# Softmax totals spread through DRAM, and layer-norm tiles moved to other units, in an attention and LoRA kernel

## The chip, the cores and the metric

The kernel runs on one core of a Trainium2 chip. The metric is the time of one execution on the device, in microseconds (us). A core has five engines that run side by side, each through its own list of instructions in order: TensorE (PE; PEld is its loading of weights), VectorE (DVE), ScalarE (ACT), GpSimd (POOL) and SyncE (SP). Here SP issues every transfer (DMA). An engine waits where its next instruction needs something that another has not finished, and everything behind that instruction waits too.

## The reference

Input x has 4 sequences of 1024 rows with 1024 columns, all in 32-bit floats. Two blocks are applied, each with a layer norm in front and the input added behind:

```python
x = x + attn(layernorm(x), wq, wk, wv, wo)      # 32 heads of 32 columns, rotary q and k, causal softmax
x = x + ffn(layernorm(x), route_w, A, Bw)       # best of 8 experts, each a low-rank pair of rank 16
```

In the attention, `probs = softmax(scores)`, `out = probs @ v`, and `out @ wo`. The kernel leaves the division by the softmax's totals until after `probs @ v`: it works with unnormalized exponentials and multiplies the result by the reciprocal of each query's total.

## The kernel before

**Units.** The work is cut into 32 units, eight per sequence (`units`, line 207). A unit is four heads of one sequence: 128 columns of q, k and v. During a unit, its scores, exponentials and products with v are made, and between these the matmuls that fill TensorE: the projections of q, k and v for the next unit, and, from the second sequence on, the output projection and the second block of one tile of 128 rows of the sequence before (`finish_steps`, line 656). Units 0 to 7 are the first sequence.

**Slots.** A unit runs through eleven slots (`SLOTS`, line 26). Nine of them make scores of some query tiles (`score_round`, 64 queries each, tile 15 the longest). Two of them, "second" and "first", make the products with v (`apply`, line 981): "second" for the later half of the queries of the unit before (block 1), "first" for the earlier half of the queries of this unit (block 0). After each slot, `fill` takes steps from `todo` up to a share of their cost; a projection step costs 1 and takes 0.86 us. The fillers of unit u are the list `between[u]`. Steps of cost 0 stand in the same list and are issued when they are reached. `postponed` (line 224) holds actions that are due after so much further cost.

**Softmax on VectorE.** Per query tile: scores are copied from PSUM to SBUF by ScalarE (L417), POOL adds the mask on the diagonal (L420), VectorE finds the largest of each row (L438, L459), ScalarE exponentiates (L467), and VectorE transposes in blocks of 32x32 (L492). The products `av` (L573) need all the transposes of their block. `av` lies in the same PSUM tile as the scores (`ps_s`, one buffer), so the next scores wait until VectorE has multiplied `av` by the reciprocals (L593).

**The totals.** `join_sums` (line 525) adds two halves of the totals (L534) and takes reciprocals (L535). For each of 512 queries and 4 heads there is one number, with queries on the partitions; `av` has head columns on the partitions and queries along the row. So POOL copies each number 32 times side by side (`by`, 128x512, L537). `spread_sums` (line 542), called after the `av` matmuls have been issued, turns `by` by four TensorE transposes (L547), and ScalarE copies the result from PSUM (L548). `join_sums` is called as soon as the last transposes of the block have been issued, a slot before the products.

**Layer norm.** `Norm` (line 233) holds the eight row tiles of one sequence: `load` brings a tile, `find` computes mean and variance on VectorE (L175 to L179) and one power on POOL (L181), `scale` normalizes in place on VectorE (L186), `turn` transposes with eight TensorE transposes and copies to `xnT` (L198 to L202). For the second sequence this happens in units 5 to 7: tiles 0 to 4 are loaded at the head of unit 5; tiles 0 and 1 are scaled in unit 5, 2 to 5 in unit 6, 6 and 7 in unit 7 (lines 855 to 865 and 808 to 810). In the class, `scale(t)` for the first sequence finds tile t + 1 before it scales tile t; for the second it finds t + 1 after.

**The DMA queue.** All transfers stand in SP's one queue in program order: chunks of weights (`load_chunk`, four buffers, each load issued after the use that frees its buffer), `vd` (v written to DRAM and read back in another layout, `spread_values`, line 500), x, results. The queue stops at the first transfer whose source or buffer isn't ready.

Of the kernel before, what the change touches and what calls it, by code (L numbers as in the profile page):

```python
# [14 lines left out]
P = 128  # L15
# [56 lines left out]
def tile_preln_attn_then_top1_lora(  # L72
# [50 lines left out]
    nc.sync.dma_start(eye_sb, eye)  # L123

    def load_x(b, t, tag="row"):
        xr = big.tile([P, D], F32, tag=tag, name=f"x_{b}_{t}", bufs=COUNT[tag])
        nc.sync.dma_start(xr, x[b, t * P : (t + 1) * P, :])
        return xr
# [7 lines left out]
    x_first = [load_x(0, t) for t in range(2)]  # L136
# [25 lines left out]
    sign_sb = const.tile([P, 1], F32, name="sign_sb")  # L162

# [68 lines left out]

    class Norm:

# [10 lines left out]
        def load(self, *tiles):  # L245
            u = self.b * NG
            for t in tiles:
                n = self.homes.get(t)
                if not n:
                    self.x[t] = load_x(self.b, t)  # L250
                    continue
                dsts = qTs if n == "q" else kTs
                if u not in dsts:
                    dsts[u] = big.tile([P, S], F32, tag="qkT", name=f"{n}T_{u}", bufs=4)
                self.x[t] = dsts[u]
                nc.sync.dma_start(dsts[u], x[self.b, t * P : (t + 1) * P, :])
# [268 lines left out]
    def join_sums(u, blk):  # L525


        if (u, blk) in bys or any((u, t) in places for t in range(blk * QT, (blk + 1) * QT)):
            return
        den = dens.pop((u, blk)).rearrange("p (t c) h -> p c t h", c=2)  # L530
        rec = small.tile([P, TB, HG], F32, tag="rec", name=f"rec_{u}_{blk}", bufs=2)
        for i in range(P // SQ):
            rows, other = slice(i * SQ, (i + 1) * SQ), slice((i ^ 1) * SQ, ((i ^ 1) + 1) * SQ)
            nc.vector.tensor_tensor(rec[rows], den[rows, i % 2], den[other, i % 2], ALU.add)  # L534
        nc.vector.reciprocal(rec, rec)  # L535
        bys[u, blk] = by = big.tile([P, TB, P], F32, tag="by", name=f"by_{u}_{blk}")
        nc.gpsimd.tensor_copy(  # L537
            by.rearrange("p t (h d) -> p t h d", d=HD),
            rec.unsqueeze(3).to_broadcast([P, TB, HG, HD]),
        )  # L540

    def spread_sums(u, blk):

        by = bys.pop((u, blk))
        pt = bank([P, TB, P], f"pr_{u}_{blk}")
        for i in range(TB):
            nc.tensor.transpose(pt[:, i, :], by[:, i, :], eye_sb)  # L547
        nc.scalar.copy(by, pt)  # L548
        return by.rearrange("p t k -> p (t k)")
# [239 lines left out]
    def change_steps(u, norm, project, tail, held):  # L789
# [32 lines left out]
    for u, (b, g) in enumerate(units):  # L822
# [13 lines left out]
        if u + 1 < len(units) and g + 1 == NG:  # L836
# [306 lines left out]
```

## Time and profile before

| | |
|---|---|
| median of 3 runs | 2755.46 us (2751.7 to 2759.22) |
| the profiled execution | 2747.7 us |
| its span, first to last instruction | 2745.9 us |
| TensorE busy | 2682.2 us (98%) |
| VectorE busy | 2126.7 us (77%) |
| ScalarE busy | 1755.0 us (64%) |
| POOL busy | 638.1 us (23%) |
| granted TensorE clock, mean | 0.998 |
| four transposes of `by` (L547) | 64 blocks, 256 instructions, 42.2 us busy |
| ScalarE's copy of `by` (L548) | 64, 586 ns each |
| POOL's copy of `by` (L537) | 64, 612 ns each |

Busy time counts matmuls as one pipelined stretch; an instruction's own duration is longer than the time that it keeps the next one from starting. In a row of a timeline, the first number is the start in us, the second the length, and a bracket at the end is the idle time of that engine just before, with the instruction that ended it. "x3" means that three like instructions were merged into the row.

### The profile page before, as it was taken

To read this page: it belongs to the slowest core of one execution; us is meant where nothing else is said; L and a number is where in the kernel's file an instruction comes from. 1 tells how busy PE (TensorE), PEld (TensorE's weight loads), DVE (VectorE), ACT (ScalarE), POOL (GpSimd) and SP (SyncE) were. 2 spreads that over 40 slices of the span, in tenths; PEclk is the share of its full clock that TensorE was granted. 3 is DMA by queue.
4 is the path that set the end of the run, shared out by engine and by line. 5 is a ranking of instruction groups with operands and counts; after the bars stand their busy time and mean duration, and the time that the engine had idled before them with its cause. 6 is when DMAs were issued, how large, how long until landed. Compare 5 with 4: busy or idle time off the path is not lost.

```text
span 2745.9 us, 84082 instructions
## 1 busy us (share of the span) xinstructions
PE 2682.2 (98%) x35328; PEld 1322.0 (48%) x35328; DVE 2126.7 (77%) x4198; ACT 1755.0 (64%) x5033; POOL 638.1 (23%) x900
## 2 busy tenths in 40 slices
PE   8999999899999999989999999998999999999998
PEld 5444444444445444445444454444544444544445
DVE  4888889887777877887777778788777777778655
ACT  2877777876666676666666666666566666666521
POOL 2222223222222222222222222222222222222000
PEclk9999999999999999999999999999999999999999
DMA  3222232325444455551654444565255544446421
GB/s 118 52 56 56 56 94 56 78 56 150 131 135 114 121 141 142 151 171 43 175 145 122 135 110 121 149 165 146 63 157 150 138 128 128 115 119 196 129 67 55
DMA packets 448012, 317.86 MB, mean 116 GB/s; under 512 B 150289, under 2 KB 371729, under 8 KB 447633
## 3 DMA queue, kind: packets, MB, share of 16 engines
q1 hardware_dynamic: 447632, 312.47, 41.6%
q8 instruction: 278, 4.55, 0.7%
q14 instruction: 102, 0.83, 0.1%
HBM read 262.59 MB, written 49.81 MB: 114 GB/s over the span
## 4 chain that ended last, share of the span: by engine, by line
PE 80%; DVE 14%; ACT 2%; DMA 1%; POOL 1%; issue 1%; SPq 0%; POOLq 0%; DVEq 0%; ACTq 0%
PE po L690 14%; PE pq L313 14%; PE pk L313 13%; PE pv L313 12%; PE s L406 11%; PE av L573 9%; DVE top L438 4%; DVE pr L492 4%; PE ph L712 2%; PE pf L751 2%; DMA chunk<-in_wo 1%; DVE both L459 1%; PE pr L547 1%; ACT pr L417 1%; PE pt_f L198 1%
## 5 line engine op out<-in xcount | busy, mean ns | idle before, releaser
L467 ACT ACTIVATE pr<-pr,both 128x256 f32<-128x256 f32 (+15 forms) x2048 | 1045.1, 519 | 58.0 <-DVE both L459 57.9
L438 DVE TENSOR_REDUCE top<-pr 128x2 f32<-128x960 f32 (+15 forms) x768 | 651.1, 894 | 251.5 <-POOL pr L420 250.9
L417 ACT COPY pr<-s 128x640 f32<-128x640 f32 (+14 forms) x544 | 525.3, 1017 | 492.3 <-PE s L406 491.7
L492 DVE STREAM_TRANSPOSE pr<-pr 128x1024 f32<-128x1024 f32 (+11 forms) x768 | 664.3, 907 | 33.3 <-ACT pr L467 30.1
L420 POOL TENSOR_TENSOR pr<-pr,causal_sb 128x128 f32<-128x128 f32 x512 | 238.0, 472 | 1070.6 <-ACT pr L417 1062.4
L313 PE MATMUL pv<-xnT,wv 128*128 128x512 f32 x1024 | 484.1, 600 | 0.0
L313 PE MATMUL pq<-xnT,wq 128*128 128x512 f32 x1008 | 476.8, 600 | 0.6 <-ACT xnT L200 0.6
L313 PE MATMUL pk<-xnT,wk 128*128 128x512 f32 x1008 | 475.9, 601 | 0.0
L406 PE MATMUL s<-kT,qT 32*32 32x256 f32 (+4 forms) x17408 | 393.0, 385 | 10.7 <-ACT pr L417 7.2
L467 ACT ACTIVATION_READ_ACCUMULATOR pr<-pr,both 128x1 f32 x2048 | 400.8, 196 | 0.0
L690 PE MATMUL po<-chunk,attn 128*128 128x512 f32 x736 | 376.3, 597 | 4.0 <-DMA chunk<-in_wo 4.0
L406 PEld LDWEIGHTS s<-kT,qT 32*32 32x32 f32 x17408 | 187.2, 103 | 267.2 <-issue 101.8
L313 PEld LDWEIGHTS pk<-xnT,wk 128*128 128x128 f32 x1008 | 181.3, 190 | 234.8 <-issue 234.6
L313 PEld LDWEIGHTS pq<-xnT,wq 128*128 128x128 f32 x1008 | 182.6, 191 | 224.0 <-issue 221.8
L313 PEld LDWEIGHTS pv<-xnT,wv 128*128 128x128 f32 x1024 | 185.7, 190 | 217.2 <-issue 212.9
L573 PE MATMUL av<-pr,vals 64*32 64x256 f32 (+3 forms) x12288 | 273.2, 320 | 11.7 <-DVE pr L492 11.6
L573 PEld LDWEIGHTS av<-pr,vals 64*32 64x32 f32 x12288 | 215.5, 106 | 119.9 <-issue 54.5
L459 DVE TENSOR_TENSOR both<-top 32x4 f32<-32x4 f32 (+3 forms) x1152 | 213.4, 185 | 23.7
L690 PEld LDWEIGHTS po<-chunk,attn 128*128 128x128 f32 x736 | 135.2, 190 | 168.0 <-issue 149.6
L548 ACT COPY by<-pr 128x512 f32<-128x512 f32 x64 | 37.5, 586 | 260.5 <-PE pr L547 260.5
L593 DVE TENSOR_TENSOR at<-av,by 128x256 f32<-128x256 f32 x128 | 48.1, 417 | 158.1 <-ACT by L548 158.0
L690 PE MATMUL po<-wo,attn 128*128 128x512 f32 x256 | 116.7, 597 | 0.0
(87 smaller groups left out, 1705.8 us busy)
## 6 DMA issues: line engine op xcount, KB each, us to landing
chunk<-in_wo SPq DMA_DIRECT2D x368, 256.0 KB, 3.6
vals<-vd SPq DMA_DIRECT2D x256, 128.0 KB, 4.5
x<-in_x SPq DMA_DIRECT2D x58, 512.0 KB, 6.0
wq<-in_wq SPq DMA_DIRECT2D x32, 512.0 KB, 4.0
wk<-in_wk SPq DMA_DIRECT2D x32, 512.0 KB, 4.0
wv<-in_wv SPq DMA_DIRECT2D x32, 512.0 KB, 4.2
vd<-vT SPq DMA_DIRECT2D x128, 128.0 KB, 4.8
out_y<-x SPq DMA_DIRECT2D x32, 512.0 KB, 2.8
```

The lines of the kernel that those rows point to most:

```text
L313: nc.tensor.matmul(at["p"], lhsT=wt[:, c, :], rhs=xnTs[b, tb][:, c, :], start=(c == 0), stop=(c == NC - 1),)
L406: nc.tensor.matmul(sc[i * SQ : (i + 1) * SQ, h, at : at + w].rearrange("p (j k) -> p j k", k=SQ), lhsT=of_q[rows, 2 * t + half], rhs=of_k[ ...
L417: nc.scalar.copy(pr[:, :, k0 : k0 + w], sc[:, :, at : at + w])
L420: nc.gpsimd.tensor_tensor(diagonal, diagonal, causal_sb.unsqueeze(1).to_broadcast([P, HG, SQ]), ALU.add)
L438: nc.vector.tensor_reduce(top[:, k, h : h + step], places[u, t][:, h : h + step, :], AX.X, ALU.max, negate=True,)
L459: nc.vector.tensor_tensor(dst[rows], src[rows], src[other], op)
L467: nc.scalar.activation(pr[:, h, :], pr[:, h, :], AF.Exp, bias=tops[u, t][:, h : h + 1], accum_out=dens[u, t // QT][:, t % QT, h : h + 1],)
L492: nc.vector.transpose(pr, pr)
L573: nc.tensor.matmul(avs[half][h * HD : (h + 1) * HD, t0:, :], lhsT=v[rows, j, h * HD : (h + 1) * HD], rhs=rhs, start=(j == 0), stop=(j == n ...
L690: nc.tensor.matmul(st["po"], lhsT=lhsT, rhs=rhs, start=(c == start), stop=(c == stop))
L712: nc.tensor.matmul(ph, lhsT=st["ynT"][:, c, :], rhs=w[:, c - i * RA, :], start=(c == 0), stop=(c == NC - 1),)
L751: nc.tensor.matmul(pf, lhsT=st["whT"], rhs=rhs, start=True, stop=True)
```

## The change

1. From the second sequence on (24 units, 48 blocks), the reciprocals are no longer spread by POOL, TensorE and ScalarE. VectorE transposes them in blocks of 32x32 (`turned`, one 128x32 instruction), four small stores put them in DRAM (`there`, 16 rows of 128 bytes each), and four loads bring them back, each row of 512 numbers repeated on 32 partitions (`by`). Stores are due after 2.0 of further step cost, loads after 5.0; `spread_sums` issues what is still left. In the first sequence the old way stays. The reciprocals now live in one constant tile, `rec_sb`, whose unused columns are set to zero once.
2. The tiles of the second sequence are loaded, found and scaled one at a time: tiles 0 to 3 in units 1 to 4, tiles 4 and 5 in unit 5, tiles 6 and 7 in unit 6. Tiles 5 and 6 lie in two half tiles each (`Two`) in the buffers of the weight chunks. Unit 7 only turns tiles 4 to 7.
3. At the start, x's first tile is loaded ahead of the identity matrix, and `scale` for the first sequence finds the next tile after scaling; for the second sequence `scale` no longer finds the next tile.

```diff
-    nc.sync.dma_start(eye_sb, eye)
...
-    x_first = [load_x(0, t) for t in range(2)]
+    x_first = [load_x(0, 0)]
+    nc.sync.dma_start(eye_sb, eye)
+    x_first.append(load_x(0, 1))
...
+    rec_sb = const.tile([P, 2, SQ], F32, name="rec_sb")
+    nc.vector.memset(rec_sb, 0.0)
...
+                if n == "chunk":
+                    self.x[t] = Two([])
+                    for cols in (slice(0, HALF), slice(HALF, D)):
+                        part = big.tile([P, HALF], F32, tag="chunk", name=f"x_{self.b}_{t}", bufs=4)
+                        nc.sync.dma_start(part, x[self.b, t * P : (t + 1) * P, cols])
+                        self.x[t].parts.append(part)
+                    continue
...
-                self.find(k + 1 if self.b == 0 else k)
-                normalize(self.x[k], self.x[k], self.moments.pop(k))
+                self.find(k)
+                moments = self.moments.pop(k)
+                for part in getattr(self.x[k], "parts", [self.x[k]]):
+                    normalize(part, part, moments)
                 self.scaled += 1
-                if self.b == 1:
+                if self.b == 0:
                     self.find(k + 1)
...
-        den = dens.pop((u, blk)).rearrange("p (t c) h -> p c t h", c=2)
-        rec = small.tile([P, TB, HG], F32, tag="rec", name=f"rec_{u}_{blk}", bufs=2)
+        den = dens.pop((u, blk)).rearrange("p (t c) h -> p c h t", c=2)
+        rec = rec_sb[:, blk, : HG * TB].rearrange("p (h t) -> p h t", t=TB)
...
-        nc.vector.reciprocal(rec, rec)
-        bys[u, blk] = by = big.tile([P, TB, P], F32, tag="by", name=f"by_{u}_{blk}")
-        nc.gpsimd.tensor_copy(
-            by.rearrange("p t (h d) -> p t h d", d=HD),
-            rec.unsqueeze(3).to_broadcast([P, TB, HG, HD]),
-        )
+        nc.vector.reciprocal(rec_sb[:, blk, : HG * TB], rec_sb[:, blk, : HG * TB])
+        if units[u][0] == 0:
...
+            bys[u, blk] = by, None
+            return
+        turned = small.tile([P, SQ], F32, tag="recT", name=f"recT_{u}_{blk}", bufs=2)
+        nc.vector.transpose(turned, rec_sb[:, blk])
+        there = dram.tile([HG * TB, P // SQ, SQ], F32, tag="recs", name=f"recs_{u}_{blk}")
+        by = big.tile([P, TB * P], F32, tag="by", name=f"by_{u}_{blk}")
+
+        def put():
+            for i in range(P // SQ):
+                nc.sync.dma_start(there[:, i], turned[i * SQ : i * SQ + HG * TB])
+
+        def get():
+            for h in range(HG):
+                of_h = there[h * TB : (h + 1) * TB]
+                nc.sync.dma_start(
+                    by[h * HD : (h + 1) * HD],
+                    bass.AP(of_h.tensor, of_h.offset, [[0, HD], [1, TB * P]]),
+                )
+
+        left = [put, get]
+        bys[u, blk] = by, left
+        for cost in (2.0, 5.0):
+            postponed.append([cost, lambda: left and left.pop(0)()])
...
-        by = bys.pop((u, blk))
...
+        by, left = bys.pop((u, blk))
+        if left is None:
...
+        while left:
+            left.pop(0)()
+        return by
...
-        out += [*chains[:2], turning(4), scaling(6), *chains[2:6], turning(5), scaling(7)]
-        out += [*chains[6:11], turning(6), *chains[11:16], turning(7)]
-        return out + chains[16:]
+        for t, n in zip(range(TB, NT), (3, 4, 4, 4)):
+            out += [*chains[:n], turning(t)]
+            del chains[:n]
+        return out + chains
...
-                norm = Norm(b + 1, {0: (5,), 1: (6,), 2: (7,)})
+                norm = Norm(b + 1, {0: (7,)}, {5: "chunk", 6: "chunk"})
+                for t, (unit, at) in enumerate(((1, 24), (2, 24), (3, 24), (4, 24), (5, 12), (5, 36))):
+                    steps = between[unit]
+                    for k, step in enumerate((norm.load, norm.find, norm.scale)):
+                        steps.insert(at - 8 + 5 * k, Step(lambda step=step, t=t: step(t), 0.0))
+                for at, step in (
+                    (own["q", 0][0], Step(lambda norm=norm: norm.load(6), 0.0)),
+                    (own["q", 1][0], norm.finding(6)),
+                    (own["q", 1][3], norm.scaling(6)),
+                    (own["v", 1][5], norm.finding(7)),
+                    (own["v", 1][7], norm.scaling(7)),
+                ):
+                    behind(last_v, at, step)
                 for t, at in enumerate((("k", 1), ("k", 1), ("k", 1), ("v", 1))):
                     behind(last_v, own[at][(1 + 3 * t) % NC], norm.turning(t))
-                behind(last_v, own["v", 1][6], norm.scaling(5))
-                behind(last_v, own["v", 1][3], norm.finding(5))
-                behind(last_v, own["k", 0][4], norm.scaling(4))
-                behind(last_v, own["q", 1][2], norm.scaling(3))
-                behind(last_v, own["q", 0][2], norm.scaling(2))
-                for t in (1, 0):
-                    between[-2].insert(10 + 16 * t, norm.scaling(t))
-                between[-2].insert(0, Step(lambda norm=norm: norm.load(*range(TB + 1)), 0.0))
```

More of the change, by code (lines that the diff above doesn't have):

```diff
@@ L231, in do_postponed, with __init__, __getitem__ @@
                 item[1]()
+    class Two:
+        def __init__(self, parts):
+            self.parts = parts
+        def __getitem__(self, key):
+            rows, cols = key
+            k, at = divmod(cols.start, HALF)
+            return self.parts[k][rows, at : at + cols.stop - cols.start]
     class Norm:
@@ L534, in join_sums @@
             nc.vector.tensor_tensor(rec[rows], den[rows, i % 2], den[other, i % 2], ALU.add)
-        nc.vector.reciprocal(rec, rec)
-        bys[u, blk] = by = big.tile([P, TB, P], F32, tag="by", name=f"by_{u}_{blk}")
-        nc.gpsimd.tensor_copy(
-            by.rearrange("p t (h d) -> p t h d", d=HD),
-            rec.unsqueeze(3).to_broadcast([P, TB, HG, HD]),
-        )
-    def spread_sums(u, blk):
-        by = bys.pop((u, blk))
[L545 to L549, printed above, removed]
+        nc.vector.reciprocal(rec_sb[:, blk, : HG * TB], rec_sb[:, blk, : HG * TB])
@@ new lines, in join_sums @@
+        if units[u][0] == 0:
+            by = big.tile([P, TB, P], F32, tag="by", name=f"by_{u}_{blk}")
+            nc.gpsimd.tensor_copy(
+                by.rearrange("p t (h d) -> p t h d", d=HD),
+                rec.rearrange("p h t -> p t h").unsqueeze(3).to_broadcast([P, TB, HG, HD]),
+            )
[3 more added lines that the diff above has]
+        nc.vector.transpose(turned, rec_sb[:, blk])
@@ new lines, in join_sums @@
+        there = dram.tile([HG * TB, P // SQ, SQ], F32, tag="recs", name=f"recs_{u}_{blk}")
[9 more added lines that the diff above has]
+                    bass.AP(of_h.tensor, of_h.offset, [[0, HD], [1, TB * P]]),
+                )
@@ new lines, in join_sums @@
+        left = [put, get]
+        bys[u, blk] = by, left
+        for cost in (2.0, 5.0):
+            postponed.append([cost, lambda: left and left.pop(0)()])
+    def spread_sums(u, blk):
+        by, left = bys.pop((u, blk))
+        if left is None:
+            pt = bank([P, TB, P], f"pr_{u}_{blk}")
+            for i in range(TB):
+                nc.tensor.transpose(pt[:, i, :], by[:, i, :], eye_sb)
+            nc.scalar.copy(by, pt)
+            return by.rearrange("p t k -> p (t k)")
+        while left:
+            left.pop(0)()
+        return by
```

## The prediction

> **What bounds the kernel now.** I read the page first: busy times, chain, groups. Then TensorE's waits, the timeline of one steady unit, the first change of sequence, and the DMA issues. A unit is one pass of the main loop: 4 heads of one sequence; 0 to 7 are the first sequence, and each later sequence also carries the finishing matmuls of the one before.
>
> From the page:
>
> ```profile
> PE 2682.2 (98%) x35328; PEld 1322.0 (48%) x35328; DVE 2126.7 (77%) x4198; ACT 1755.0 (64%) x5033; POOL 638.1 (23%) x900
> ```
>
> TensorE is idle for 64 us of 2745.9. From its waits (total, times, longest):
>
> ```profile
> PE av L573 <- DVE pr L492: 11.6, 2, 9.1
> PE pt_a L198 <- DVE x L186: 9.8, 2, 9.1
> PE s L406 <- ACT pr L417: 7.2, 6, 1.7
> ```
>
> The 9.1 of the second row is the start; that of the first lies at 539 to 548, in unit 7. From 720 to 1110, in the second sequence's steady units (82.3 us each), TensorE has no wait at all: there, each us of its work is a us of time. The timeline of TensorE, then of VectorE, around one block of such a unit (start, us, instruction, [idle before]):
>
> ```profile
> 1421.70 2.35 PE L573 MATMUL av<-pr,vals 64*32 64x256 f32 x128
> 1423.98 0.65 PE L547 MATMUL pr<-eye_sb,by 128*128 128x128 f32 x4
> 1424.47 1.02 PE L313 MATMUL pv<-xnT,wv 128*128 128x512 f32 x2
> ```
>
> ```profile
> 1415.88 2.08 DVE L438 TENSOR_REDUCE top<-pr 128x2 f32<-128x896 f32 x2 [1.20 <-POOL pr L420]
> 1425.29 0.75 DVE L593 TENSOR_TENSOR at<-av,by 128x256 f32<-128x256 f32 x2 [2.63 <-ACT by L548]
> ```
>
> The four transposes of `by` hold TensorE from 1423.98 to 1424.47: 0.49 us (0.50 for the other block at 1465.54). The multiplication that needs them starts 1.3 us after the av matmuls end.
>
> The first sequence is different: in the second half of its units VectorE has no gap but one of 1.19 us, and TensorE sits at its heels. Unit 5 already normalizes a tile in that place (VectorE 432.20 to 434.56), and TensorE pays:
>
> ```profile
> 445.90 1.49 PE L406 MATMUL s<-kT,qT 32*32 32x384 f32 x64 [1.38 <-DVE at L593]
> 456.95 1.44 PE L406 MATMUL s<-kT,qT 32*32 32x256 f32 x64 [1.74 <-ACT pr L417]
> 548.09 5.90 PE L573 MATMUL av<-pr,vals 64*32 64x256 f32 x128 [9.05 <-DVE pr L492]
> ```
>
> A unit without that tile shows no wait and 0.92 us at the first two places. The third row is the pile-up: the tiles left for the end of units 6 and 7. What it does to the clock is in the table by stage (columns: stretch, length, busy PE, PEld, DVE, ACT, POOL, granted clock):
>
> ```profile
> 540.00:546.00 6.00, 0.00 (x0) 0.00 (x0) 5.82 (x13) 3.79 (x13) 0.37 (x2) 0.66 0.01 1
> 546.00:552.00 6.00, 3.91 (x72) 3.05 (x80) 5.85 (x14) 2.20 (x10) 2.17 (x5) 0.50 0.01 3
> ```
>
> These av matmuls take 5.90 us, where they take 3.69 at 400.42: 2.2 more.
>
> **Part 1, the totals by DRAM** (48 blocks, units 8 to 31). Removed per block: TensorE 0.495 us; a ScalarE copy (0.586); a POOL copy (0.612). 48 x 0.495 = 23.8. Five blocks lie where TensorE waits anyway (two at each change into the third and fourth sequence, and the last one): 43 x 0.495 = **-21.3**. The ScalarE copy is on no path of a steady unit: nothing. The POOL copy sits ahead of a mask that VectorE then waits for (the [1.20] above): VectorE gains that, which pays only at the two later changes, where VectorE is busy 38 of 40 us and TensorE waits 2.6, 2.3, 1.6 and 0.7. I take 1 us each, **-2** (0 to 4). Added on VectorE: a 128x32 transpose; the rows for 128x128 (0.30) and 256 (0.40) give an estimate of 0.2, hidden in a steady unit's idle.
>
> Added on SP: 4 stores of 2 KB and 4 loads of 64 KB per block, 0.33 to 0.43 us each to issue, 1.6 per group. The first store waits for VectorE, the first load for the stores' landing. No row has either transfer. Bounds for one landing, from the issues:
>
> ```profile
> chunk<-in_ra SPq DMA_DIRECT2D x24, 136.0 KB, 2.2
> vd<-vT SPq DMA_DIRECT2D x128, 128.0 KB, 4.8
> causal_sb<-in_causal SPq DMA_DIRECT2D x4, 4.0 KB, 5.8
> ```
>
> I take 2.2 for either leg. The last row is nearest in size, but it was issued behind some 4.5 MB of loads at the start; SP's later queue is mostly idle. The same round trip is in the kernel for `vd`: SP waits there 33 times, 33.2 us in all.
>
> Follow the block above. SP is free from 1415.9 (its next load waits until 1419.2), the totals are ready at 1414.9; stores issued by 1417.5, landed 1419.7. The loads come after five steps of cost, behind a weight chunk at 1420.1: issued 1420.4 to 1422.0, landed 1424.2. The av matmuls end at 1424.0, and the old path gave `by` at 1425.3: no loss. The other block: totals ready 1456.6, stores to 1458.2, landed 1460.4, loads to 1462.0, landed 1464.2; needed 1465.5. What stands behind these waits on SP is the router's chunks: the one of 1454.3 goes out at 1458.5, that of 1456.9 at 1462.3; both are used after 1466. Hidden, with about 3 us to spare.
>
> It isn't hidden in two places. At the changes in units 15 and 23 the store waits for totals ready at 1195.3 while three weight chunks, issued at 1190.3 to 1191.5, stand behind it. They go out at 1197, land 3.6 later, and TensorE wants the first at 1197.9: up to 3 us, of which I count half, since it waits for others soon after: **+3** for two. And units 8, 16 and 24 (short fills) reach the stores only at 663.8: loads land at 671.4, against 669.5 now; **+1.5** for three.
>
> Part 1: -21.3 - 2 + 3 + 1.5 = **-18.8**.
>
> [...]
>
> **Part 2, the tiles of the second sequence** (first: nothing of the amount of work changes, only the place). In units 1 to 4 each tile's find comes after VectorE's work of the 15th query tile, its scale directly behind. Adjacent pairs wait for POOL (0.67 at 409.93), so it is 3.07 us from 407.59 to 410.66. VectorE's gap of 1.19 there waits for VectorE's own totals by way of POOL, so it moves along. Unit 5 before: 2.36 us put in, TensorE lost 1.38 + 1.74 - 0.92 = 2.2. So 3.07 costs 2.9; four units **+11.6**. Bounds: 0, if the earlier place lets TensorE's idle-free first half absorb it, and 3.1 plus 2.2 of lost clock. I take the unit-5 row: same tile, same half.
>
> Unit 5 keeps two: tile 4 ahead of the av matmuls' next wait, free; tile 5 in halves late in the unit, 1.64 + 1.0, +2.5, against 0.88 + 2.2 = 3.1 now. Unit 7's stall: between 533.8 and 548 VectorE now does 4.74 + 2.35 = 7.1 us of normalizing; then only tile 7, 3.07. The stall of 9.05 falls by 4.0 to 5.0, enough to keep the 2.2 of clock, and 0.32 goes. Before: 3.1 + 9.05 + 2.2 + 0.32 = 14.7. After: 11.6 + 2.5 + 7.2 = 21.3. Part 2: **+6.6**. Moved with them: each tile's load (0.33 to 0.57 us of SP, which in the first sequence issues 17 DMAs a unit and stands idle otherwise; it lands about 6 us later, in a 12 us lead; tiles 5 and 6 as two loads of half the size), its POOL power (0.55 at 409.35, between other POOL work) and, in unit 7, the tile turns, one matmul step earlier or later: nothing each. Without that lead, VectorE would stand at the find.
>
> [...]
>
> **Part 3, the start.** x's first tile is issued at 0.74, not 1.18 (-0.4), and its scale no longer stands behind the second tile's statistics (6.60 to 8.15): scale at 6.9 instead of 8.22, so the first transposes begin at 7.8 and not 9.08. The weights follow in the old order. **-1.3** (0 to -1.8). A memset of 64 columns lies beside the first load.
>
> **Sum:** -18.8 + 6.6 - 1.3 = -13.5. The profiled execution took 2747.7 us (span 2745.9): 2734.2. The median shown is 2755.46, 7.8 above it: **2742**.
>
> **Rivals.**
> - *The moved tiles are absorbed.* Part 2 loses the 11.6: -25, 2730. For it: VectorE idles 2.8 and 3.5 us in the first half of each unit. Against it: unit 5.
> - *The stalls in units 1 to 4 drop the clock.* 4 x 2.2 on top: 2751. For it: 135.18, after 2.60 us. Against it: 1.73 and 1.74 cost no clock.
> - *Slower: the round trip by DRAM ends after the av matmuls in every unit.* VectorE then stands at the multiplication, the PSUM tile stays held, and TensorE's next scores wait. In the first block that starts when two landings take over 9.3 us (from 1417.5 with 1.6 of issue and 0.75 of multiplying to 1429.2). At 5.8 each it is 2.3 us there and 1.8 in the other block, 24 x 4.1 = 98: 2840. For it: the causal row. Against it: every large transfer of the middle lands in 2.2 to 4.8.
> - *TensorE's gain comes back as waits on VectorE or ScalarE* (no gain from part 1's slots): 2763. Against it: 77% and 64% busy.
>
> **Chances.** Forecast 0.50, absorbed 0.20, clock 0.13, slow round trip 0.12, no gain 0.05. About 0.3%, 8 us, is what a measurement can tell from no change: faster means below 2747. Of the forecast's 0.50 I put 0.08 above that. Faster 0.42 + 0.20 = 0.62; same 0.08 + 0.13 + 0.05 = 0.26; slower 0.12. The range takes in the first three cases with their bounds: 2726 to 2760.
>
> **What the new profile would show.** Steady units of 81.3 us; SP's waits for the `recs` stores 48 times, a few us each at most; VectorE's wait at the multiplication on PE or DMA, short. Units 1 to 4 with 2 to 3 us of new TensorE waits on `at` and `pr`, the stall in unit 7 at about 5. I am wrong if the multiplication waits for DMA by more than 5 us in steady units, or if units 1 to 4 keep their length.

## The result, and the profile after

| | before | after |
|---|---|---|
| median, 14 runs each | 2749.74 us (2745.66 to 2759.22) | 2750.8 us (2745.76 to 2754.09) |
| ratio | | 0.9999, 95% interval 0.9991 to 1.0007 |
| the profiled execution | 2747.7 us | 2752.48 us |
| its span | 2745.9 us | 2750.7 us |
| its granted clock, mean | 0.998 | 0.992 |

No difference that can be measured. The granted clock is the one number of the table that moved. It isn't chance: 29 runs of the kernel before lie at 0.994 to 0.998 (mean 0.9960), the 14 runs of the changed one at 0.991 to 0.994 (mean 0.9926). Taken over 2750 us, the clock lacks some 11 us per run before and some 20 after.

From the page of the changed kernel:

```profile
PE 2680.1 (97%) x35136; PEld 1307.2 (48%) x35136; DVE 2143.1 (78%) x4249; ACT 1727.5 (63%) x4985; POOL 608.5 (22%) x852
```

192 matmuls are gone, yet TensorE's busy time fell by only 2.1 us: matmuls in a drop of the clock were busy for longer, as shown below (the same 64 took 2.35 us in a drop and 1.48 at full clock).

**The steady units** are shorter, as forecast, but by 0.79 us and not by 0.99 (81.54 from 82.33). The timeline of TensorE behind the av matmuls of one block:

```profile
1510.35 2.35 PE L626 MATMUL av<-pr,vals 64*32 64x256 f32 x128
1512.63 1.13 PE L337 MATMUL pv<-xnT,wv 128*128 128x512 f32 x2
1513.59 1.02 PE L743 MATMUL po<-chunk,attn 128*128 128x512 f32 x2
```

The four transposes no longer stand between av and pv. But the first pv group now holds TensorE from 1512.63 to 1513.59, 0.96, where the like group at 1516.17 holds it 0.86 (to 1517.03). Before, the pv group behind the transposes held it 0.86 too (1424.47 to 1425.33). So here the first group after av takes 0.10 us more, and before, that lay in the transposes: they held TensorE 0.49, but only 0.39 of it goes with them.

VectorE at another block of the same unit, and what SP's queue waited for (total, times, longest):

```profile
1544.81 0.21 DVE L570 STREAM_TRANSPOSE recT<-rec_sb 128x32 f32<-128x32 f32 x1
1553.93 0.76 DVE L646 TENSOR_TENSOR at<-av,by 128x256 f32<-128x256 f32 x2 [1.52 <-PE av L626]
```

```profile
SPq L576 <- DVE recT L570: 252.8, 48, 13.0
SPq L581 <- DMA recs<-recT: 32.1, 46, 2.4
```

The multiplication waits for TensorE's av and not for the loads: the round trip is hidden, as it was worked out. From 700 to 1110 and from 1300 to 1790 TensorE has no wait. The second row is SP's wait for the stores to land, 0.7 us a block. The first is the price in the queue: SP stands 252.8 us in all before a store that VectorE hasn't made ready.

**The first sequence.** TensorE's timeline in units 1 to 5 and 7:

```profile
181.49 2.35 PE L430 MATMUL s<-kT,qT 32*32 32x384 f32 x64 [2.70 <-DVE at L646]
252.01 1.61 PE L430 MATMUL s<-kT,qT 32*32 32x384 f32 x64 [2.71 <-DVE at L646]
322.61 1.48 PE L430 MATMUL s<-kT,qT 32*32 32x384 f32 x64 [2.79 <-DVE at L646]
333.66 1.44 PE L430 MATMUL s<-kT,qT 32*32 32x256 f32 x64 [1.74 <-ACT pr L441]
393.17 2.37 PE L430 MATMUL s<-kT,qT 32*32 32x384 f32 x64 [2.70 <-DVE at L646]
461.81 2.46 PE L430 MATMUL s<-kT,qT 32*32 32x384 f32 x64 [2.53 <-DVE at L646]
559.82 5.91 PE L626 MATMUL av<-pr,vals 64*32 64x256 f32 x128 [4.15 <-DVE pr L516]
```

In units 1 to 4 stand four waits of 2.70 to 2.79 on `at`, where the forecast had 2.9 us a unit in two waits (on `at` and on `pr`). But look at the lengths: the same 64 matmuls take 1.48 in the third row and 2.35 in the first. By stage (stretch, length, busy PE, PEld, DVE, ACT, POOL, granted clock):

```profile
180.00:184.00 4.00, 2.51 (x65) 1.35 (x66) 4.00 (x6) 0.81 (x4) 0.00 (x0) 0.69 0.17 66
184.00:188.00 4.00, 4.00 (x45) 1.64 (x48) 3.92 (x8) 1.81 (x2) 0.45 (x1) 0.88 0.02 4
```

Over these 8 us the clock lacks 4 x (0.31 + 0.12) = 1.72 us. In finer stretches it is 0.50 from about 181.6 to 185.0 and 1.00 on both sides. Units 2 to 4 have a stretch that lacks the same (0.65 and 0.92; 0.89 and 0.68; 0.65 and 0.93). In unit 3 it begins at 335.15, behind the 1.74 of the fourth row; the longest wait, the 2.79 of the third, had no drop behind it. Summed over the whole span, the clock lacks 6.8 us before (one drop at 135, three in the stall of 548) and 20.5 us after, one at the very end left out: 4 drops became 12. By the means above, this profile of before has fewer drops than its runs have on average.

**The changes of sequence.** SP's queue at the third change, and TensorE:

```profile
1867.22 0.33 SPq L700 DMA_DIRECT2D chunk<-in_wo  x1
1873.16 2.69 SPq L576 DMA_DIRECT2D recs<-recT  x4
1875.95 1.32 SPq L700 DMA_DIRECT2D chunk<-in_wo  x3
```

```profile
1878.64 2.07 PE L743 MATMUL po<-chunk,attn 128*128 128x512 f32 x2 [3.11 <-DMA chunk<-in_wo]
1898.25 3.62 PE L743 MATMUL po<-chunk,attn 128*128 128x512 f32 x4 [1.79 <-DMA chunk<-in_wo]
```

SP stands still from 1867.6 to 1873.2 before the stores; the three weight chunks behind them go out at 1875.95, and TensorE waits 3.11 for the first. Three of the twelve drops lie here (clock 0.75, 0.50 and 0.90 from 1876 to 1888, then 0.81 and 0.77 from 1896).

**Where the time went.** Each block computes its reciprocals once, 64 in all, so their starts are milestones that all kernels share. How far each kernel is behind (+) or ahead (-) of the profile of before, in us:

| reciprocal (start before) | after | totals_only | tiles_only | tiles_early | queue_late | tiles_gap | totals_all | all_three | best |
|---|---|---|---|---|---|---|---|---|---|
| 2nd (136.5) | 0.0 | +0.3 | 0.0 | +0.5 | -0.1 | -0.2 | +4.7 | +4.2 | -0.6 |
| 10th (400.8) | +15.8 | +1.8 | +13.7 | -1.7 | +0.2 | -0.3 | -1.0 | -1.3 | +1.3 |
| 18th (699.6) | +11.4 | +2.7 | +9.9 | -7.4 | -5.1 | -12.9 | -2.6 | -13.1 | -10.0 |
| 30th (1195.0) | +6.4 | -1.7 | +9.9 | -12.5 | -9.9 | -17.9 | -6.8 | -17.6 | -14.1 |
| 31st (1240.6) | +8.8 | +3.0 | +10.7 | -8.0 | -10.1 | -14.1 | -4.7 | -18.2 | -14.2 |
| 46th (1870.2) | +2.4 | -3.5 | +11.7 | -14.2 | -16.5 | -20.2 | -11.1 | -24.4 | -19.7 |
| 47th (1915.9) | +8.9 | +0.7 | +14.7 | -10.6 | -16.2 | -13.4 | -7.9 | -24.6 | -20.3 |
| 64th (2661.7) | +3.1 | -5.7 | +14.2 | -16.1 | -21.7 | -19.4 | -13.3 | -30.8 | -25.1 |

The column "after" shows where: 15.8 lost in units 1 to 4, 4.4 given back in units 5 to 8, then 0.39 gained per block, with 2.5 and 6.5 lost at the second and third change (30th to 31st, 46th to 47th). The other columns are the experiments.

### The profile page after: what moved, and what is told of

Same layout as the page of the kernel before. It is cut to its first block, busy times and chain, and to the rows that moved or that the text cites. A ratio compares the mean times of both kernels' runs of the same rounds, so it can differ in the third digit from the quotient of the medians.

```text
span 2750.7 us, 84042 instructions
## 1 busy us (share of the span) xinstructions
PE 2680.1 (97%) x35136; PEld 1307.2 (48%) x35136; DVE 2143.1 (78%) x4249; ACT 1727.5 (63%) x4985; POOL 608.5 (22%) x852
## 4 chain that ended last, share of the span: by engine, by line
PE 79%; DVE 13%; ACT 2%; DMA 2%; POOL 1%; issue 1%; SPq 1%; POOLq 0%; DVEq 0%; ACTq 0%
PE po L743 14%; PE pq L337 14%; PE pk L337 13%; PE pv L337 12%; PE s L430 11%; PE av L626 8%; DVE pr L516 4%; DVE top L462 4%; PE ph L765 2%; PE pf L804 2%; DMA chunk<-in_wo 1%; ACT pr L441 1%; DVE both L483 1%; PE pt_f L201 1%; ACT pr L491 1%
## 5 line engine op out<-in xcount | busy, mean ns | idle before, releaser
L430 PE MATMUL s<-kT,qT 32*32 32x256 f32 (+4 forms) x17408 | 398.5, 390 | 21.1 <-DVE at L646 13.4
L743 PE MATMUL po<-chunk,attn 128*128 128x512 f32 x736 | 383.7, 607 | 9.0 <-DMA chunk<-in_wo 8.6
L483 DVE TENSOR_TENSOR both<-top 32x4 f32<-32x4 f32 (+3 forms) x1152 | 204.9, 178 | 23.8
L375 POOL TENSOR_TENSOR qT<-qT,swapq 128x512 f32<-128x512 f32 x64 | 81.7, 1277 | 146.3 <-DVE swapq L371 146.3
```

Source lines behind the costliest of these rows:

```text
L375: nc.gpsimd.tensor_tensor(dst[:, cols], dst[:, cols], other, ALU.add)
L430: nc.tensor.matmul(sc[i * SQ : (i + 1) * SQ, h, at : at + w].rearrange("p (j k) -> p j k", k=SQ), lhsT=of_q[rows, 2 * t + half], rhs=of_k[ ...
L483: nc.vector.tensor_tensor(dst[rows], src[rows], src[other], op)
L743: nc.tensor.matmul(st["po"], lhsT=lhsT, rhs=rhs, start=(c == start), stop=(c == stop))
```

## The experiments

| run | median (runs) | before beside it | ratio, 95% interval |
|---|---|---|---|
| totals_only | 2740.79 (6) | 2751.73 | 0.9962 (0.9950 to 0.9974) |
| tiles_only | 2761.02 (5) | 2751.73 | 1.0032 (1.0020 to 1.0044) |
| tiles_early | 2736.32 (5) | 2751.73 | 0.9944 (0.9932 to 0.9956) |
| ladder | 2757.96 (1) | 2751.73 | |
| queue_late | 2731.1 (6) | 2752.37 | 0.9920 (0.9906 to 0.9935) |
| tiles_gap | 2730.04 (6) | 2752.37 | 0.9916 (0.9901 to 0.9931) |
| totals_all | 2736.32 (6) | 2752.37 | 0.9940 (0.9927 to 0.9954) |
| all_three | 2721.82 (5) | 2752.37 | 0.9893 (0.9877 to 0.9909) |
| best | 2724.26 (4) | 2750.11 | 0.9904 (0.9887 to 0.9920) |
| start_only | 2751.13 (1) | 2750.11 | |

The theory after the result: part 1 gains, part 2 and the changes give it back, the drops of the clock included. The rival: part 1 gains nothing, and the tiles cost nothing.

### totals_only and tiles_only: each part alone

totals_only is the kernel before with the totals of the diff alone (`rec_sb`, `join_sums`, `spread_sums`); tiles_only is the kernel before with the tiles alone (`Two`, `Norm`, the places of the steps). The lines that each takes over:

```diff
+        if units[u][0] == 0:
...
+        left = [put, get]
...
+        for cost in (2.0, 5.0):
+            postponed.append([cost, lambda: left and left.pop(0)()])
```

```diff
+                norm = Norm(b + 1, {0: (7,)}, {5: "chunk", 6: "chunk"})
+                for t, (unit, at) in enumerate(((1, 24), (2, 24), (3, 24), (4, 24), (5, 12), (5, 36))):
```

> The kernel before with the first part of the change alone (totals by DRAM from the second sequence on). Theory A (gain given back: each steady unit is 0.8 us shorter, the chunk queue loses some of it at the two later changes of sequence): 6 to 10 us faster than before, 0.9965 to 0.998; steady units of 81.5 us; waits of TensorE on weight chunks of 3 to 5 us at each later change. Theory B (the slots of the four transposes come back as waits somewhere, nothing reaches the end): 0.9995 to 1.0005, steady units of 82.3.

> The kernel before with the second part alone (tiles of the second sequence one per unit). Theory A: 10 to 14 us slower, 1.0036 to 1.005, with four TensorE waits of 2.7 us on the multiplication by the totals in units 1 to 4 and a granted clock below 0.95 in 20 us behind at least three of them; unit 7's wait 4 instead of 9 us. Theory B: within 3 us of before, since the work moved is the same work.

Measured: the totals alone gain 0.38%, a little more than theory A, and the tiles alone cost 0.32%, a little less than it. The two ratios multiply to 0.9994, which agrees with the result within the intervals. The totals alone also show the late chunks at the two changes:

```profile
1198.96 1.13 PE L721 MATMUL po<-chunk,attn 128*128 128x512 f32 x2 [1.57 <-DMA chunk<-in_wo]
1873.04 1.92 PE L721 MATMUL po<-chunk,attn 128*128 128x512 f32 x2 [3.41 <-DMA chunk<-in_wo]
```

The tiles alone make the same waits in units 1 to 4, and show that a drop doesn't always follow. In unit 2:

```profile
253.52 1.48 PE L425 MATMUL s<-kT,qT 32*32 32x384 f32 x64 [2.67 <-DVE at L612]
264.58 1.44 PE L425 MATMUL s<-kT,qT 32*32 32x256 f32 x64 [1.75 <-ACT pr L436]
```

The clock stays at 1.00 through both. Behind the equal waits in units 1, 3 and 4 it drops, 1.7 us lost each time. In these three units the next wait on ScalarE is then 0.22 or none instead of 1.75, so that most of the drop is taken from slack. That is why each unit loses 3.2 to 3.5 us in tiles_only, drop or none: 3.2 in unit 2 without, 3.4 to 3.5 in the others with one.

### tiles_early: the same tiles a quarter of a unit earlier

```diff
-                for t, (unit, at) in enumerate(((1, 24), (2, 24), (3, 24), (4, 24), (5, 12), (5, 36))):
+                for t, (unit, at) in enumerate(((1, 12), (2, 12), (3, 12), (4, 12), (5, 12), (5, 36))):
```

> The changed kernel with tiles 0 to 3 twelve steps earlier in their units, where VectorE idles before and after the multiplication by the totals of the other block. Theory A (the place decides, and the clock falls only behind the long waits): the four waits of 2.7 us and their lost clock go, 12 to 16 us off the changed kernel: 0.9945 to 0.996 of before. Rival (VectorE's work in a first-sequence unit costs TensorE wherever it stands): no better than 3 us off the changed kernel.

Measured: 2736.3, 0.56% faster than before. All four waits are gone; this is what is left (unit 4, then unit 5, whose tile still stands late):

```profile
386.72 1.44 PE L430 MATMUL s<-kT,qT 32*32 32x256 f32 x64 [0.97 <-ACT pr L441]
444.44 1.57 PE L430 MATMUL s<-kT,qT 32*32 32x384 f32 x64 [2.66 <-DVE at L646]
```

The amount of work on every engine is that of the changed kernel. At the 10th reciprocal the kernel is 17.5 us ahead of the changed one (-1.7 against +15.8). So it was the place of the tiles in the unit that cost.

### ladder: useless work of four sizes on VectorE in that place

The kernel before, with a memset and one or two transposes of a spare tile at step 24 of units 1 to 4; they change no result.

```diff
+                for unit, widths in ((1, (128,)), (2, (768,)), (3, (512, 512)), (4, (1024, 512))):
+                    between[unit].insert(24, Step(lambda widths=widths: idle_work(widths), 0.0))
```

> The kernel before with useless VectorE work (a memset of 128x1024 and transposes of a spare tile) at step 24 of units 1, 2, 3 and 4, growing: some 0.9, 1.5, 2.0 and 2.5 us. It computes what the kernel before computes. Theory A: in each unit the next scores but one wait for VectorE's multiplication by the work put in less 1.0 us of slack, and the rest of it shows as a longer wait at the next unit's first scores; the granted clock falls only where one wait exceeds about 2.5 us, so in none of them or in unit 4 alone. Rival: the clock falls behind waits of 1 to 2 us as well.

The work took 1.22, 1.89, 2.37 and 2.90 us. TensorE:

```profile
181.03 1.49 PE L406 MATMUL s<-kT,qT 32*32 32x384 f32 x64 [0.26 <-DVE at L593]
192.09 1.44 PE L406 MATMUL s<-kT,qT 32*32 32x256 f32 x64 [1.75 <-ACT pr L417]
249.44 1.48 PE L406 MATMUL s<-kT,qT 32*32 32x384 f32 x64 [0.91 <-DVE at L593]
260.50 1.44 PE L406 MATMUL s<-kT,qT 32*32 32x256 f32 x64 [1.75 <-ACT pr L417]
318.69 1.49 PE L406 MATMUL s<-kT,qT 32*32 32x384 f32 x64 [1.40 <-DVE at L593]
329.75 1.44 PE L406 MATMUL s<-kT,qT 32*32 32x256 f32 x64 [1.74 <-ACT pr L417]
386.77 1.49 PE L406 MATMUL s<-kT,qT 32*32 32x384 f32 x64 [1.93 <-DVE at L593]
```

The waits on `at` are the work less 0.96 to 0.98 each time: in this place TensorE has 0.97 us of slack to VectorE and pays every us beyond. In the first three units the next wait grows besides, from 0.92 to 1.75. The clock, behind the 1.40 and 1.74 of unit 3 and behind the 1.93 of unit 4:

```profile
332.00:336.00 4.00, 4.00 (x42) 1.64 (x41) 3.89 (x9) 4.00 (x12) 0.92 (x2) 1.00 0.01 4
388.00:392.00 4.00, 4.00 (x28) 1.63 (x6) 4.00 (x5) 1.93 (x2) 0.46 (x1) 0.57 0.06 20
```

A drop follows the 1.93, and one the 1.75 at 260.50 (0.76 and 0.81 in the two stretches behind it), but none the equal waits at 192.09 and 329.75. So theory A's limit of 2.5 us is wrong, its rival is right, and no length of a single wait between 1.7 and 2.7 decides it.

What tells such waits apart stands in the clock's records in the traces of before and of the changed kernel. In each of the two, all drops begin whole steps of 3.413 us apart: in the changed kernel, those of 181.55, 253.23 and 335.15 are 21 and 24 steps apart, before, those of 135.68 and 541.87 are 119. These steps, the grid in what follows, have another place in each of the two: counted from each start, 135.68 and 181.55 are 13.44 steps apart. TensorE's idle time within one step goes with the drops better than the length of a wait does. The same wait at 135 us, first before and then in the changed kernel:

```profile
135.18 5.85 PE L573 MATMUL av<-pr,vals 64*32 64x256 f32 x128 [2.60 <-DVE pr L492]
135.09 4.22 PE L626 MATMUL av<-pr,vals 64*32 64x256 f32 x128 [2.61 <-DVE pr L516]
```

The steps of the grid around it, two before and three in the changed kernel (TensorE's busy time is the number behind the comma, the granted clock the third from the end):

```profile
132.27:135.68 3.41, 0.81 (x9) 0.18 (x8) 3.41 (x5) 3.41 (x15) 0.00 (x0) 1.00 0.00 0
135.68:139.10 3.42, 3.42 (x68) 1.78 (x72) 3.22 (x10) 1.56 (x8) 1.85 (x2) 0.50 0.02 5
```

```profile
130.35:133.77 3.42, 2.13 (x5) 0.58 (x4) 3.26 (x8) 3.42 (x14) 0.91 (x2) 1.00 0.00 0
133.77:137.18 3.41, 2.10 (x64) 1.35 (x72) 3.25 (x9) 3.36 (x14) 0.30 (x1) 1.00 0.02 5
137.18:140.59 3.41, 3.41 (x76) 1.93 (x60) 3.26 (x10) 0.92 (x4) 1.56 (x2) 1.00 0.00 0
```

Before, the whole 2.60 lies in one step, and the next has half the clock (0.50). In the changed kernel it is split into 1.29 and 1.31, and nothing follows. In these two profiles, from 20 us on and in steps at full clock: more than 2.0 us idle in a step had a drop behind it 12 times of 12, 1.7 to 2.0 us 2 times of 7, less than 1.7 us none of 1561 times. What tells these 2 from the other 5 stays open.

### queue_late: the weights of a change ahead of the stores

tiles_early, and in the unit before each change the stores and loads of the second block are due later, so that three weight chunks are issued first.

```diff
-        for cost in (2.0, 5.0):
+        late = blk == 1 and units[u][1] == NG - 2 and units[u][0] + 1 < B
+        for cost in (6.0, 7.0) if late else (2.0, 5.0):
```

> The kernel is tiles_early (tiles 0 to 3 a quarter of a unit earlier), and in units 14 and 22 the stores and loads of the reciprocals of the second block are due after 6.0 and 7.0 of further cost, not 2.0 and 5.0, so that the weight chunks of the next change stand ahead of the stores in SP's queue and not behind them. Theory (the weights of a change are late because they stand behind a store that waits for VectorE): the waits of po for chunk at the two later changes (1.7 and 0.5 us at the second, 2.9 at the third in tiles_early) go, and the clock fall behind the 2.9 with them: 3 to 6 us, 2731 to 2734 where tiles_early gives 2736. Rival A (the chunks wait for something else, such as the buffer that the use before frees): the waits stay, 2736. Rival B: the reciprocals now come too late, the multiplication waits for DMA at these two places for some 3 us each, and the next scores behind it: 2737 to 2742.

Measured: 2731.1. SP's queue and TensorE at the third change:

```profile
1849.74 0.80 SPq L701 DMA_DIRECT2D chunk<-in_wo  x2
1852.23 0.33 SPq L701 DMA_DIRECT2D chunk<-in_bw  x1
1854.29 2.60 SPq L576 DMA_DIRECT2D recs<-recT  x4
```

```profile
1866.02 1.13 PE L744 MATMUL po<-chunk,attn 128*128 128x512 f32 x2 [0.41 <-DMA chunk<-in_wo]
```

The chunks go out before the stores, the waits of 1.68 and 2.86 that tiles_early had for the first chunk are gone, 1.4 to 1.8 are left further on, and the clock has no drop at either change. Between the 30th and 31st reciprocal it gains 0.1 where tiles_early loses 4.5; between the 46th and 47th it loses 0.3 where tiles_early loses 3.7. The loads come in time. Of these 8.0 us, 2.4 are waits that are shorter; the rest goes with the drops, of which tiles_early has three between 1170 and 1226 and one at 1862, 1.7 us each before slack. But only the drops at 1190.23 and 1862.65 stand behind waits for a chunk. Those at 1173.16 and 1220.95 stand behind a 2.12 for ScalarE and a 2.26 for VectorE, and queue_late has these waits as well (2.01 and 2.27) without a drop. So up to 3.4 of the 8.0 need not be the edit: it can be where the steps of 3.413 us fell, an estimate from these two drops. The medians, over several runs each, differ by 5.2.

### tiles_gap: one tile per unit, and tile 7 in unit 7

```diff
-                for t, (unit, at) in enumerate(((1, 12), (2, 12), (3, 12), (4, 12), (5, 12), (5, 36))):
+                for t, (unit, at) in enumerate(((0, 12), (1, 12), (2, 12), (3, 12), (4, 12), (5, 12))):
...
-                    (own["v", 1][5], norm.finding(7)),
-                    (own["v", 1][7], norm.scaling(7)),
...
+            if t == 6:
+                out[-n:-n] = [norm.finding(7), norm.scaling(7)]
```

> The kernel is tiles_early with tiles 0 to 5 one per unit in units 0 to 5, all at the early place (tile 5 is no longer in the late half of unit 5), and tile 7's find and scale in unit 7 behind the tile turn 5 instead of at the end of unit 6. Theory (a stall is set by where in VectorE's row of a unit a tile stands, not by how many tiles there are): the 2.66 at unit 5 and the 1.66 behind it go, the stalls of 2.15 and 5.58 in unit 7 shrink to under 3 together, and with them the clock falls of these places: 8 to 12 us, 2725 to 2728 where tiles_early gives 2736. Rival (unit 7 has no idle place on VectorE, so the tile is paid for wherever it stands, and unit 0, which has its own fillers, pays for tile 0): 2733 to 2738.

Measured: 2730.0, ratio 0.9916 against 0.9944 for tiles_early, 0.28% or 7.7 us (6.3 by the medians), a little under the expected 8 to 12. Unit 5 has no wait but the usual 0.96; of unit 7's stalls this is left:

```profile
523.61 1.83 PE L430 MATMUL s<-kT,qT 32*32 32x256 f32 x64 [2.13 <-ACT pr L441]
537.38 0.64 PE L626 MATMUL av<-pr,vals 64*32 64x256 f32 x8 [1.08 <-DVE pr L516]
```

5.58 became 1.08 (and 0.25 a few matmuls on). At the 18th reciprocal it is 5.5 us ahead of tiles_early. (6.7 lost at the third change are more than the 3.7 of tiles_early: a wait of 3.19 for a chunk and the drops behind it.)

### totals_all: the totals by DRAM in the first sequence too

```diff
-        if units[u][0] == 0:
+        if units[u][0] < 0:
```

> The kernel is tiles_early with the totals spread by DRAM in the first sequence as well (16 more blocks). Theory: TensorE loses 0.39 us per block where it is the bound, 14 x 0.39 = 5.5, and VectorE no longer waits 1.19 us per unit for the mask behind POOL's copy, which helps in units 5 to 7 where VectorE sets the end: 5 to 9 us, 2727 to 2731 where tiles_early gives 2736. Rival (in the first sequence the fillers between the two places are too short, so that the loads go out late, and the multiplication waits for them some 2 us in each unit): no gain or a loss, 2736 to 2745.

Measured: 2736.3, the same as tiles_early. The theory's gain is there: from the 2nd to the 10th reciprocal it gains 5.6 us, tiles_early 2.2. It is paid for ahead and behind. The rival's late loads come in unit 0 alone, not in each unit. There, on VectorE, and on TensorE behind it:

```profile
113.92 0.76 DVE L646 TENSOR_TENSOR at<-av,by 128x256 f32<-128x256 f32 x2 [7.35 <-DMA by<-recs]
```

```profile
114.83 2.37 PE L430 MATMUL s<-kT,qT 32*32 32x384 f32 x64 [4.63 <-DVE at L646]
```

The loads are issued only at 110.55 to 112.25. This is the prediction's slow rival, in one block of 64. And at the first change the chunks now stand behind stores as well (a wait of 2.44 at 655.43), 3.4 us between the 17th and 18th reciprocal.

### all_three: the three edits together

```diff
+        late = blk == 1 and units[u][1] == NG - 2 and units[u][0] + 1 < B
...
+        if units[u][0] < 0:
...
+                for t, (unit, at) in enumerate(((0, 12), (1, 12), (2, 12), (3, 12), (4, 12), (5, 12))):
```

> All three edits on top of tiles_early: chunks ahead of the stores at the later changes, tiles at the early place in units 0 to 5 and tile 7 in unit 7, totals by DRAM in all sequences. Theory: the three gains lie at different places and add: 2712 to 2722 where tiles_early gives 2736. Rival (the gains of the second and the third edit are the same VectorE time in units 5 to 7, and only one is had): 2724 to 2730.

Measured: 2721.8, 1.07% faster than before (0.91 to 1.23%): the slow end of what was expected, and the fastest median of the study. The chunks now go ahead of the stores at all three changes. From 1150 to 1950, the second and the third change, TensorE's waits for them are:

```profile
PE po L744 <- DMA chunk<-in_wo: 2.2, 3, 1.0
```

The gains do add: by the medians 14.5 us off tiles_early, where the three edits alone gave 5.2, 6.3 and 0.0. At the end of the profile it is 30.8 us ahead of before, 14.7 more than tiles_early. The wait in unit 0 is still there (4.45 at 114.61).

### best: the old way in unit 0 alone

```diff
-        if units[u][0] < 0:
+        if u == 0:
```

> The kernel is all_three with the old way of the totals (POOL, TensorE, ScalarE) kept in unit 0 alone. Theory: the 4.5 us for which the scores at 114.6 wait there, since the loads of unit 0's first block are issued too late, go, and the clock fall behind them; two blocks lose their 0.39 us each: 3 to 5 us, 2717 to 2719 where all_three gives 2722. Rival (unit 0's time is given back anyway: all_three was 1.3 us ahead of the kernel before again at the tenth reciprocal): no change, 2721 to 2723.

Measured: 2724.3, ratio 0.9904 against 0.9893, with intervals that overlap: no gain. The 4.8 us are won (at the 2nd reciprocal -0.6 against +4.2), and by the 10th they are lost again. Part of it shows as pauses of TensorE that nothing in the trace releases:

```profile
349.21 0.74 PE L430 MATMUL s<-kT,qT 32*32 32x320 f32 x7 [1.96 <-issue]
```

There are three of 2.0 to 2.3 at this place of units 3 to 5, against two of 1.3 and 1.9 in all_three, and behind this one the clock drops. What makes these pauses stays open.

### start_only: part 3 alone

```diff
-    x_first = [load_x(0, t) for t in range(2)]
+    x_first = [load_x(0, 0)]
+    nc.sync.dma_start(eye_sb, eye)
+    x_first.append(load_x(0, 1))
...
-                self.find(k + 1 if self.b == 0 else k)
+                self.find(k)
```

> The kernel before with part 3 alone: x's first tile ahead of the identity matrix, and in the first sequence the next tile's statistics behind the scaling. As predicted: the first transposes begin 1.3 us earlier and the end comes 1.3 us earlier. Rival (from the profile of the changed kernel): the first wait shrinks by 1.4 us, but the first unit is then bound by something else, and at the first reciprocal 0.6 us or less are left.

TensorE's first matmuls, and the second group that waits for a scaled tile:

```profile
7.80 1.97 PE L199 MATMUL pt_a<-eye_sb,x 128*128 128x128 f32 x8 [7.80 <-DVE x L187]
40.08 1.06 PE L199 MATMUL pt_a<-eye_sb,x 128*128 128x128 f32 x8 [1.18 <-DVE x L187]
```

The first transposes begin 1.28 us earlier, at the very 7.8 that was worked out. 0.6 are lost again by the first reciprocal (0.45 of them at 40.08, where the wait is 1.18; before has one of 0.73 instead, at 36.37), so the rival is right at that place; by the 10th reciprocal the kernel is 1.3 ahead, which is the forecast. One run of 2751.13 can't tell 1.3 us from none: in its profile the third change, which the edit doesn't touch, takes 3.3 us more than in the profile of before. Two drops stand there, at 1892.58 and 1906.23, with waits of 2.10 and 2.27; the profile of before has 1.73 and 2.26 at these places and no drop.

## Why the prediction was right in its range and wrong in its sign

The range (2726 to 2760) holds the 2750.8. The forecast, faster by 13.5, does not hold: by the medians of 14 runs the change is worth +1.1 us, by the two profiles +4.8. Only because the forecast was hung on a median of three runs, which lay 5.7 us above that of 14, did 2742 come as near as 8.8. By its steps, all from the profiles (18.3 us between -13.5 and +4.8):

- **The slot of the transposes: mis-sized.** 43 blocks at 0.495 were counted, and 0.39 each came: 4.5 us less. The sum took the whole time between av and the next matmul; 0.10 of it belongs to the group that now follows av.
- **Units 1 to 4: the waits nearly right, the clock wrong.** 2.9 a unit was read off unit 5; the one unit of tiles_only without a drop lost 3.2. The loss in the changed kernel is 15.8 where +11.6 was counted. The rival "the stalls drop the clock" was dismissed since waits of 1.73 and 1.74 cost no clock. But waits of over 2 us were nearer to the 2.60 at 135.18, behind which the same trace had a drop. This is the step that failed: the sum has no term for drops of the clock in these units or at the changes, and all four units had one, unit 3 behind a wait of 1.74. Its price was less than the rival's 2.2, though. Three of the four stand ahead of a wait that shrinks, and those units lost 1.9, 3.3 and 3.8 us (unit 1 is spared the drop that before has at 135.68). Unit 3 lost 6.8: its drop stands behind the second wait, where nothing took it up, and a pause of 1.19 at 289.77 that nothing in the trace releases comes on top.
- **The changes: the mechanism right, the clock wrong again.** Stores that wait for VectorE with three chunks behind them were foreseen, "up to 3 us, of which I count half". TensorE waited 3.11 for the first chunk at the third change. But TensorE's waits there became only 0.5 and 2.0 us longer in sum; the drops (one at the second change, three at the third, none in the profile of before) are 6.8. The two changes cost 2.9 and 6.9 us (2.5 and 6.5 in the table, and 0.39 that the block would have gained); +1 was counted for both, the 2 us of VectorE's relief in it. That is 8.7 us more, about as much as units 1 to 4 and the transposes together. queue_late shows that the late chunks, and the drops behind them, go with the order in the queue. The drop at the second change (1191.90) isn't one of these: it follows a wait for ScalarE that before has too, and longer, without a drop (first row the changed kernel, second before).

```profile
1191.30 1.54 PE L201 MATMUL pt_a<-eye_sb,x 128*128 128x128 f32 x8 [2.12 <-ACT yn L203]
1184.96 1.14 PE L198 MATMUL pt_a<-eye_sb,x 128*128 128x128 f32 x8 [2.60 <-ACT yn L200]
```

So this part can befall the kernel before too, as start_only's profile shows.

- **Unit 5 and unit 7: right in sum, in part by luck.** -0.6 was forecast for unit 5 and +0.1 came. For unit 7, 14.7 - 3.1 = 11.6 was to become 7.2, that is -4.4, and -4.5 came: a stall of 4.15 where 5.0 was forecast, but a second one of 2.51, each with a drop.
- **The round trip by DRAM: right.** It is hidden in every steady unit, and the multiplication waits for av. totals_all shows the rival's 4.6 us where the filling work is too short.
- **The short fills: right in size** (+1.5 for three; about +0.8 in unit 8, nothing in the others). **The start:** -1.3 at the first matmul, -0.6 left at the first reciprocal, 0.0 at the second.

So the rival with 2751 names the number that was measured, and its mechanism is at work; that the number fits is luck. Of the eight drops more than in the profile of before, only half lie in units 1 to 4, where the rival put them, and slack took up most of what three of these cost; the rest of the loss is at the changes and in the slots. Part 1 alone, forecast at -18.8, gained 0.38%, some 10.5 us, and 5.6 by the two profiles. In the profiles, the mis-sized slot is 4.5 of the difference of 13.2, and the two changes (4.7 and 4.2 in the table's rows, and 0.39 each) are the rest.

## What to carry to other kernels

An engine that is 77% busy can still have a stretch in which TensorE is right behind it. Here work moved into that stretch cost its length less 0.97 us of slack in every unit, and the same work a quarter of a unit earlier cost nothing: look for the place before counting the work. Where a change makes a new TensorE wait of 2 us or more, count a drop of the clock as a risk on top, here 1.7 us, unless slack behind it takes it up; it came behind a part of such waits only (three of the four of about 2.7 us in tiles_only). And since waits of 2.12 and 2.26 in tiles_early had a drop and the like ones of 2.01 and 2.27 in queue_late had none, one profile's drops are no measure of an edit: compare medians. When a transfer that waits for an engine is put into an in-order queue, list what stands behind it and who needs that first.

## What the runs showed of the hardware

- In the traces of before and of the changed kernel, each drop of the granted clock, but for those that the end of the execution cuts short, was 0.50 for 3.413 us, 1.7 us lost; the wait of 9.05 before had three in a row (541.87 to 552.11), that of 3.11 after two (1877.98 to 1884.81), that of 4.15 after one (560.43 to 563.85). A drop followed some waits and spared equal ones: in ladder 1.75 at 260.50 but not 1.75 at 192.09, in tiles_only 2.66 at 391.15 but not 2.67 at 253.52.
- In each of these two traces all drops begin whole steps of 3.413 us apart. Of the steps at full clock from 20 us on, those in which TensorE idled over 2.0 us had a drop behind them 12 times of 12, those with 1.7 to 2.0 us 2 times of 7, those with less none of 1561 times.
- The first 128-row group of matmuls after the av matmuls (64 rows by 32 columns) took 0.10 us longer than the same group elsewhere, 0.96 at 1512.63 against 0.86 at 1516.17 in the changed kernel.
- The stores landed sooner than the 2.2 that the prediction took from the trace of before, 1.4 us, the loads as assumed, 2.2 (last column: median us from issue to landing):

```profile
by<-recs SPq DMA_DIRECT2D x192, 64.0 KB, 2.2
recs<-recT SPq DMA_DIRECT2D x192, 2.0 KB, 1.4
```
